# Seven block products for one more batch, x loaded batch by batch, and the first Wk load over two queues, in a cross-attention kernel

## The chip, the cores and the metric

The kernel runs on one core of a Trainium2 chip. The metric is device time in microseconds (us) for one execution. The engines of the core are named as the profile names them: PE (TensorE, matmuls), PEld (its weight loads), DVE (VectorE), ACT (ScalarE), POOL (GpSimd) and SP (SyncE, which here only issues DMAs). Each engine runs its own instructions strictly in the order in which the program wrote them, and waits where an instruction needs a result of another engine.

## The reference

Cross-attention of 16 batches of 256 rows (x, width 256) over 77 context keys each (width 192), with 8 heads of width 256, a residual and a layer norm. Everything is float32.

```python
Q = (img_embed @ Wq).reshape(B, -1, H, D).transpose(0, 2, 1, 3)
K = (sent_embed @ Wk).reshape(B, -1, H, D).transpose(0, 2, 1, 3)
V = (sent_embed @ Wv).reshape(B, -1, H, D).transpose(0, 2, 1, 3)
score = jnp.einsum('bhqd,bhkd->bhqk', Q, K) / math.sqrt(D)
score = jnp.where(mask, score, -jnp.inf)
attn = jax.nn.softmax(score, axis=-1)
ctx = jnp.einsum('bhqk,bhkd->bqhd', attn, V).reshape(B, -1, H * D)
out = ctx @ Wo + img_embed
# then layer norm over the last axis, with gamma and beta
```

## The kernel before

**Weights first.** The kernel never forms Q, K or V. It multiplies the weights of each head ahead of time: `gA`, `gB` hold Wk·Wqᵀ per head (the 192 context rows split 128 + 64, which is what A and B mean throughout), and `uA`, `uB` hold Wv·Wo. Per batch it then needs `a` (context times g: the keys as seen from x, `prepare_a`), and `vw` (context times u: the values as seen from the output, `prepare_vw`). The first part of the kernel, up to some 42 us, loads and turns the weights and builds g and u. All of its loads but half of Wv's stand in SP's queue in program order; the very first is `wk_nat` (Wk of the heads 0 and 1), then `wq_nat`, `wk_last`, `c_sb` (context) and blocks of Wq and Wk for the other heads.

**The main loop.** A tile is 128 rows of x; a batch is two tiles (2b and 2b+1), and four batches are a group g. The loop runs over `b` from -1 to 14, and I call one pass step b. Step b computes the scores and softmax of batch b+1 (its tiles are `new`), the output product of batch b (`now`), and the layer norm of batch b-1 (`old`). The order of calls in a step is the order of the instructions on each engine; the schedule is written out by hand, and no scheduler moves anything.

In a middle step, in order:

- `scores` (PE, L300) and `shift` (DVE, L317: adds the mask and takes the row minimum out of PSUM, eight per tile).
- In every second step (`ahead`), `prepare_vw` and `prepare_a` for the next two batches (PE, L190 to L235) and their copies out (ACT). In the steps 13 and 14 (`alone`) it is `prepare_vw` of the next batch only.
- `exponential` (ACT, L338), `finish` (DVE, L505 and L508: the statistics of an old tile), `weigh` (DVE L351 and L353, then POOL L359: divides by the denominators and writes `p`).
- `differences` (POOL, L412) and `sums` (POOL, L429 to L432): the sums and differences of blocks that the seven products need. `seven` (PE, L448) makes them, and an ACT copy (L473) brings four of them from PSUM to the tile `m`; `add_seven` (DVE L497, then five POOL additions, L483) puts the blocks together in `xg`, the tile that holds x and becomes the output.
- `turn` (DVE, L369: transposes `p` into `pT`), `normalise` (DVE L547 and L576, or with `aside` ACT L570 and POOL L571, L572), and the store (SP).

**Seven products or eight.** For one batch, `p` (two tiles) times `vw` is a 2×2 block product. `seven` does it with seven products of 128 output columns in place of eight, and needs `differences(b)` of `vw` and `sums(b)` of `pT` for that. `attend` (PE, L381) does the plain product, and needs neither. `NS` says which batches take which: the batches below NS, 13 before the change, take `seven`; the batches 13, 14 and 15 take `attend` (the very last tile `attend_halves`, L397). Two more things hang on NS. `vw` is kept as four blocks, and for the batches below NS one of them is the sum that `seven` reads in place of a plain block (`t2`). And `summed_by_act(t)` lets ACT sum the exponentials as it makes them (an accumulator read, L338), except for tiles from 2·NS up to 29, for which DVE does it (TENSOR_REDUCE, L351).

The four POOL operations of `sums` are in this order, and `seven` reads s2 in its second product:

```python
nc.gpsimd.tensor_tensor(s1, a2[0], a2[1], ALU.add)
nc.gpsimd.tensor_tensor(s3, a2[0], a1[0], ALU.subtract)
nc.gpsimd.tensor_tensor(s2, a2[1], s3, ALU.add)
nc.gpsimd.tensor_tensor(s4, a1[1], s2, ALU.subtract)
...
contract(pm[:, 0], *block(pT[0][:, 0:2], b11))
contract(pm[:, 1], *block(s2, t2))
```

**The last steps.** Step 13 calls `attend` for batch 13 and normalises batch 12 `aside`. Step 14 is written apart: it calls `shift` for tile 30, `finish` for tile 26, `shift` for tile 31, `finish` for tile 27, then the softmax of both tiles, `attend` for the tiles 28 to 30 and `attend_halves` for 31, with the last normalisations between them.

**Loads of x.** x comes twice: `load_x` brings rows into `xg` (for the residual), and `load_xT` brings 32×32 blocks into `xT`, which DVE transposes later (L162) for `scores`. Group g+1 is loaded while group g is worked on: `load_x` brings two batches (512 KB) in every second step, and `load_xT` one batch in four DMAs of 64 KB, twice. With `after_pool=True` a small POOL memset (L148) stands ahead of the load, and SP waits for that.

Of the kernel before, what the change touches and what calls it, by code (L numbers as in the profile page):

```python
# [16 lines left out]
P = 128  # L17
H = 8
D = 256
EPS = 1e-05  # L20
GB = 4
# [6 lines left out]
def kernel(  # L28
# [13 lines left out]
    nc = tc.nc  # L42
    B, S, DI = x.shape
# [3 lines left out]
    NG = B // GB  # L47
# [41 lines left out]
    NH = DI // 2 // BK  # L89
    uA = const.tile([P, 5, NH, NF, BK], F32, tag="uA", name="uA")  # L90
    uB = const.tile([P, 5, NH, NF, BK], F32, tag="uB", name="uB")
    NS = B - GB // 2 - 1

    def of_e(u, e):
        return u[:, 3 - 2 * e : 5 - 2 * e].rearrange("p q n i c -> p (q n) i c")
# [24 lines left out]
    def load_x(g, n=None, of=QT):  # L120
        if not n:
            xg_of[g] = const.tile([P, GT, DI], F32, tag=f"xg{g}", name=f"xg_{g}")
        lo, hi = (0, GT) if n is None else (n * QT, n * QT + of)
        nc.sync.dma_start(xg_of[g][:, lo:hi], x_rows[:, g * GT + lo : g * GT + hi, :])
# [17 lines left out]
    def load_xT(g, lo=0, hi=GT, after_pool=False):  # L142


        if lo == 0:
            xT_of[g] = in_two("xT", [P, GT * NM, 2, BK], g)
        if after_pool:
            nc.gpsimd.memset(xT_of[g][:BK, lo * NM, 0, :1], 0.0)  # L148
        rows = x.rearrange("b s d -> (b s) d")[(g * GT + lo) * P : (g * GT + hi) * P, :]
        rows = rows.rearrange("(m r) (i n) -> i r m n", r=BK, i=NM)  # L150
        for i in range(NM):
            nc.sync.dma_start(
                xT_of[g][i * BK : (i + 1) * BK, lo * NM : hi * NM].rearrange(
                    "p m n q -> p m (n q)"
                ),
                rows[i],
            )
# [218 lines left out]
    def attend(t):  # L376
        b, pT = t // QT, pT_of.pop(t)
        po = ps_mm.tile([P, DI], F32, tag="mm", name=f"po_{t}")
        for n in range(NF + 1):
            for i in range(NM):  # L380
                nc.tensor.matmul(  # L381
                    po[i * BK : (i + 1) * BK],
                    pT[:, n, i],
                    vw_of[b][:, 2 - n // 2 * 2 : 4 - n // 2 * 2, n % 2, :] if n < NF else vr[:, b, :],
                    start=(n == 0),
                    stop=(n == NF),
                )
        po_of[t] = po
# [46 lines left out]
    def seven(b):  # L435
        pT = [pT_of.pop(QT * b + i) for i in range(QT)]
        vw, ss = vw_of[b], ss_of.pop(b)
        ts = ts_of.pop(b)
        pm = ps_mm.tile([P, 4, P], F32, tag="mm", name=f"pm_{b}")
        po = ps_mm.tile([P, 4, P], F32, tag="mm", name=f"po_{b}")  # L440
        t2, b21, b22, b11 = (vw[:, q] for q in range(4))
        t4, t1, t3 = (ts[:, q] for q in range(3))
        s1, s3, s2, s4 = (ss[:, i] for i in range(4))

        def contract(out, *terms, first=True, final=True):
            for n, (weight, moving) in enumerate(terms):
                for i in range(NM):
                    nc.tensor.matmul(  # L448
                        out[i * BK : (i + 1) * BK],
                        weight[:, i],  # L450
                        moving,
                        start=first and n == 0,
                        stop=final and n == len(terms) - 1,
                    )

        def block(weights, moving):
            return [(weights[:, k], moving[:, k]) for k in range(2)]

        contract(pm[:, 0], *block(pT[0][:, 0:2], b11))
        contract(pm[:, 1], *block(s2, t2))  # L460
        contract(pm[:, 2], *block(s3, t3))
        contract(pm[:, 3], *block(s1, t1))
        for i in range(QT):
            contract(flat(po[:, 2 * i : 2 * i + 2]), (pT[i][:, NF], vr[:, b, :]), final=False)
            if i == 0:
                contract(po[:, 0], *block(pT[0][:, 2:4], b21), first=False, final=False)
                contract(po[:, 1], *block(s4, b22), first=False)
            else:
                contract(po[:, 2], *block(pT[1][:, 2:4], t4), first=False)
        for i in range(QT):  # L470
            po_of[QT * b + i] = flat(po[:, 2 * i : 2 * i + 2])
        m = vwp.tile([P, 4, P], F32, tag="m", name=f"m_{b}", bufs=1)
        nc.scalar.copy(m, pm)  # L473
        m_of[b] = m
# [127 lines left out]
    with tc.tile_pool(name="wonce", bufs=1) as wp:  # L602
# [39 lines left out]
            nc.gpsimd.tensor_copy(flat(cB)[:LB, rest], flat(cB)[LB:, rest])  # L642
            nc.gpsimd.tensor_copy(cRB, cB[:, :, KM:])

        nc.sync.dma_start(wk_nat, wk[:P, : 2 * D])
        for e in range(2):
            nc.sync.dma_start(wq_nat[:, :, e * D : (e + 1) * D], wq_rows[:, :, e * D : (e + 1) * D])
        for e in range(2):
# [304 lines left out]
    def work_of(b, rest_first=False):  # L953
        g, n = b // GB + 1, b % GB
        work = [prepare_vw(b, rest_first)]
        if g < NG - 1 or g == NG - 1 and n < NF // 2:
            work.append(prepare_a(g, (n,), rest_first=rest_first))
        elif b <= NS:
            part = (0, 2) if g < NG else (2, GB)
            work.append(prepare_a(NG - 1, (NF // 2 + n % 2,), *part, rest_first))  # L960
        return work
# [18 lines left out]
    for b in range(-1, B - 1):  # L980
        old = range(max(b - 1, 0) * QT, b * QT)
        now = range(max(b, 0) * QT, (b + 1) * QT)
        new = range((b + 1) * QT, (b + 2) * QT)
        for t in new if b >= 0 else ():
            scores(t)
        for t in new if b >= 0 else ():
            shift(t)
            if b == B - 2:
                finish(t - 2 * QT)
        while behind:  # L990
            behind.pop(0)()
        g, n = (b + 1) // GB + 1, (b + 1) % GB
        if g < NG and n % 2 == 0:
            load_x(g, n, 2 * QT)
        for m in range(0, 2) if b < 0 else range(b + 2, min(b + 3, B // 2)):
            turn_last(m)
        alone = b + 1 >= B - GB // 2
        works = work_of(b + 1) if alone or n % 2 == 0 else []
        for part_A, _, _ in works:
            part_A()  # L1000
        for _, part_B, _ in works:
            part_B()
        if b == B - 2:
            exponential(new[0])
            weigh(new[0])
            turn(new[0])
            spread(old[0], old[1] + 1)
            invert(old[0], old[1] + 1, aside=old[:1])
            normalise(old[1])
            exponential(new[1])  # L1010
            weigh(new[1])
            copy_out(works)
            normalise(old[0], aside=True)
            for t in now:
                attend(t)
            finish(now[0])
            centre(now[0])
            turn(new[1])
            scale_and_store(now[0])
            break  # L1020
        for i, t in enumerate(new if b >= 0 else ()):
            exponential(t)
            if old:
                finish(old[i])
            weigh(t)
        ahead = works and not alone
        if old and not ahead:
            spread(old[0], old[-1] + 1)
        if ahead:
            copy_out(works)  # L1030
            if old:
                spread(old[0], old[-1] + 1)
            works = work_of(b + 2, rest_first=True)
            for _, part_B, _ in works:
                part_B()
            for part_A, _, _ in works:
                part_A()
        copy_out(works)
        if b + 1 < NS:
            differences(b + 1)  # L1040
        if ahead and g < NG:
            load_xT(g, n * QT, (n + 1) * QT, after_pool=True)
        if b < NS:
            if now:
                seven(b)
            if old:
                invert(old[0], old[-1] + 1)
                normalise(old[0])
            for t in new:
                turn(t)  # L1050
            if b < 0:
                for j in range(QT, GT, 2):
                    transpose_x(0, j)
                bias_of(GB, B)
            if alone or ahead:
                turn_x_and_normalise(g, n, old)
                if ahead and g < NG:
                    load_xT(g, (n + 1) * QT, (n + 2) * QT)
            else:
                behind.append(partial(turn_x_and_normalise, g, n, old))  # L1060
            if ahead:
                sums(b + 1)
            if now:
                add_seven(b)
            if b + 1 < NS and not ahead:
                sums(b + 1)
            continue
        for t in now:
            attend(t)
        invert(old[0], old[-1] + 1, aside=old[:1])  # L1070
        normalise(old[0], aside=True)
        turn(new[0])
        normalise(old[1])
        turn(new[1])
        for t in now:
            add_product(t)


    attend(last - 1)
    attend_halves(last)  # L1080
# [40 lines left out]
```

## Time and profile before

| | |
|---|---|
| median of 3 runs | 270.57 us (270.32 to 271.32) |
| profiled execution, its own time | 270.98 us |
| span in that profile | 269.2 us |
| PE busy | 262.9 us (98%) |
| DVE busy | 185.2 us (69%) |
| POOL busy | 173.2 us (64%) |
| ACT busy | 157.7 us (59%) |
| granted TensorE clock | 1.0 throughout |
| DMA | 22.69 MB, mean 84 GB/s |

The span is measured from the first to the last instruction of the profiled execution; 1.78 us of its time lie outside. Busy shares are means over the whole span. The profile's chain of work is followed back from the last instruction, and shows what the end waited for at each point.

### The profile page before, as it was taken

What the parts mean: (1) busy time and instruction counts of PE and PEld (TensorE: products, weight loads), DVE (VectorE), ACT (ScalarE), POOL (GpSimd) and SP (SyncE); (2) the same over time, 40 slices, a digit from 0 to 9 for tenths busy, and PEclk for the clock granted to TensorE, in tenths of its full rate; (3) what the DMA queues carried; (4) which work ended last, traced back from release to release, by engine and by line L of the source; (5) the groups of instructions that cost most, each with busy time, mean ns of one, the idle gap of its engine ahead of it and who ended that gap; (6) DMA issues with size and microseconds to landing.
All of it is one profiled execution on the core that took longest, in us unless ns stands there. A gap on an engine that the chain in (4) does not pass through costs nothing.

```text
span 269.2 us, 14427 instructions
## 1 busy us (share of the span) xinstructions
PE 262.9 (98%) x6090; PEld 194.3 (72%) x6090; DVE 185.2 (69%) x808; ACT 157.7 (59%) x667; POOL 173.2 (64%) x240
## 2 busy tenths in 40 slices
PE   8999999999999999999999999999999999999993
PEld 7566598954985599459954995499769967984662
DVE  1555966483574758764896379647977897799785
ACT  3243335626857555964587377738684595636772
POOL 1042005637399647995699759965999799685462
PEclk9999999999999999999999999999999999999999
DMA  6999999901500130323022400340044010100112
GB/s 193 200 204 206 325 144 171 322 9 32 130 7 2 41 82 5 69 82 94 5 62 70 110 6 14 108 123 4 6 119 122 2 44 5 44 22 22 44 41 80
DMA packets 41616, 22.69 MB, mean 84 GB/s; under 512 B 24064, under 2 KB 40528, under 8 KB 41552
## 3 DMA queue, kind: packets, MB, share of 16 engines
q1 hardware_dynamic: 41168, 20.98, 32.7%
q0 software_dynamic: 384, 0.79, 1.4%
q8 instruction: 48, 0.79, 1.2%
q14 instruction: 16, 0.13, 0.2%
HBM read 17.57 MB, written 4.19 MB: 81 GB/s over the span
## 4 chain that ended last, share of the span: by engine, by line
PE 93%; DMA 3%; DVE 1%; SPq 1%; issue 0%; DVEq 0%
PE ps L300 25%; PE pa L190 12%; PE pv L224 11%; PE po L448 11%; PE pm L448 8%; PE pa L202 6%; PE pv L235 6%; PE po L381 4%; PE pu L777 3%; PE pr L260 2%; PE pgb L838 2%; DMA c_sb<-in_ctx_dram 2%; DMA wk_blk<-in_L_xattn_Wk_dram 2%; PE pw L791 1%; PE phb L854 1%; PE pr L271 1%
## 5 line engine op out<-in xcount | busy, mean ns | idle before, releaser
L338 ACT ACTIVATE e<-s,top 128x77 f32<-128x77 f32 x256 | 85.3, 346 | 44.5 <-DVE top L317 38.2
L300 PE MATMUL ps<-a,xT 128*32 128x154 f32 x2048 | 70.1, 294 | 0.0
L300 PEld LDWEIGHTS ps<-a,xT 128*32 128x32 f32 x2048 | 66.5, 110 | 1.1 <-issue 0.4
L359 POOL TENSOR_TENSOR p<-e,rden 128x512 f32<-128x512 f32 x64 | 47.5, 768 | 29.5 <-DVE rden L353 29.4
L317 DVE CUSTOM_DVE_ANT_0 s<-ps,bias 128x77 f32<-128x77 f32 x256 | 43.6, 232 | 14.8 <-PE ps L300 14.8
L338 ACT ACTIVATION_READ_ACCUMULATOR e<-s,top 128x1 f32 x224 | 42.0, 187 | 0.0
L190 PE MATMUL pa<-cA,gA 128*32 128x308 f32 (+1 forms) x576 | 36.8, 395 | 0.0
L190 PEld LDWEIGHTS pa<-cA,gA 128*32 128x32 f32 x576 | 19.0, 110 | 20.4 <-issue 6.7
L483 POOL TENSOR_TENSOR xg<-xg,m 128x256 f32<-128x256 f32 x39 | 28.7, 736 | 6.6 <-DVE xg L497 4.6
L576 DVE SCALAR_TENSOR_TENSOR xg<-xg,rstd,bet 128x256 f32<-128x256 f32 x27 | 22.2, 821 | 14.7 <-ACT rstd L527 13.3
L224 PE MATMUL pv<-uA,cA 128*32 128x512 f32 x256 | 30.8, 595 | 0.0
L412 POOL TENSOR_TENSOR ts<-vw 128x768 f32<-128x768 f32 x13 | 24.0, 1848 | 5.9 <-ACT vw L966 5.9
L369 DVE STREAM_TRANSPOSE pT<-p 128x640 f32<-128x640 f32 x32 | 25.5, 820 | 3.4 <-POOL p L359 3.3
L966 ACT COPY vw<-pv 128x512 f32<-128x512 f32 x32 | 17.8, 584 | 15.3 <-PE pv L224 8.1
L497 DVE TENSOR_TENSOR xg<-po,xg 128x256 f32<-128x256 f32 x31 | 11.5, 405 | 14.5 <-PE po L448 13.9
L317 DVE DVE_READ_ACCUMULATOR2_ANT top<- 128x1 f32 x256 | 20.8, 81 | 0.0
L202 PE MATMUL pa<-cB,gB 64*32 64x308 f32 (+2 forms) x512 | 20.4, 387 | 0.0
L966 ACT COPY a<-pa 128x308 f32<-128x308 f32 (+1 forms) x56 | 18.9, 395 | 1.9 <-PE pa L190 0.4
L202 PEld LDWEIGHTS pa<-cB,gB 64*32 64x32 f32 (+1 forms) x512 | 11.0, 110 | 11.4 <-issue 6.2
L547 DVE SCALAR_TENSOR_TENSOR xg<-xg,mv,gam 128x256 f32<-128x256 f32 x30 | 17.5, 585 | 0.1
L235 PE MATMUL pv<-uB,cB 64*32 64x512 f32 x256 | 17.3, 597 | 0.0
L224 PEld LDWEIGHTS pv<-uA,cA 128*32 128x32 f32 x256 | 8.0, 109 | 12.5 <-issue 9.5
(119 smaller groups left out, 407.6 us busy)
## 6 DMA issues: line engine op xcount, KB each, us to landing
xT<-in_x_dram SPq DMA_DIRECT2D x52, 64.0 KB, 2.4
xg<-in_x_dram SPq DMA_DIRECT2D x6, 512.0 KB, 4.2
out_dram<-xg SPq DMA_DIRECT2D x11, 256.0 KB, 2.3
wo<-in_L_xattn_Wo_dram SPq DMA_DIRECT2D x4, 512.0 KB, 8.9
wq_blk<-in_L_xattn_Wq_dram SPq DMA_DIRECT2D x12, 128.0 KB, 4.5
out_dram<-xg SPq DMA_DIRECT2D x10, 128.0 KB, 1.7
wk_blk<-in_L_xattn_Wk_dram SPq DMA_DIRECT2D x12, 96.0 KB, 4.3
xg<-in_x_dram SPq DMA_DIRECT2D x1, 1024.0 KB, 7.9
```

What stands on the lines that cost most here:

```text
L190: nc.tensor.matmul(flat(o[i * BK : (i + 1) * BK]), gA[:, h, cols(dc, i)], flat(cA[:, batches, :]), start=not rest_first and n in opening, ...
L202: nc.tensor.matmul(flat(banks[j + k][i * BK : (i + wide) * BK]), gB[half(k), h // 2, dc * P + i * BK : dc * P + (i + wide) * BK], flat(cB[ ...
L224: nc.tensor.matmul(pv[k][i * BK : (i + 1) * BK], cA[:, b, k * BK : (k + 1) * BK], uA[:, parts, :, i], start=not rest_first, stop=rest_first,)
L235: nc.tensor.matmul(pv[k][i * BK : (i + 1) * BK], cB[half(k), b, k * BK : (k + 1) * BK], uB[half(k), parts, :, i], start=rest_first, stop=n ...
L300: nc.tensor.matmul(ps[m // 2][i * BK : (i + 1) * BK, m % 2 * 2 * S2 : (m % 2 + 1) * 2 * S2], xT_of[g][:, j * NM + m, dc], flat(a_of[g][:, ...
L317: nc.vector.tensor_tensor_reduce(s[:, h], ps[a][:, k * S2 : (k + 1) * S2], bias[:, b, :], scale=-1.0, scalar=FAR, op0=ALU.add, op1=ALU.min ...
L338: nc.scalar.activation(e[:, h], s[:, h], AF.Exp, bias=top[:, one], scale=-1.0, accum_out=den[:, one] if summed_by_act(t) else None,)
L359: nc.gpsimd.tensor_tensor(part, e_mh[:, :, :, keys], rden_mh.unsqueeze(3).to_broadcast(list(part.shape)), ALU.mult,)
L369: nc.vector.transpose(pT_of[t].rearrange("p n m q -> p m n q"), p.rearrange("p m (n k) -> p m n k", k=BK),)
L448: nc.tensor.matmul(out[i * BK : (i + 1) * BK], weight[:, i], moving, start=first and n == 0, stop=final and n == len(terms) - 1,)
L483: nc.gpsimd.tensor_tensor(to, to, what, ALU.add)
L966: nc.scalar.copy(dst, src)
```

## The change

Three things change.

- `NS` goes from 13 to 14, so that batch 13 takes `seven` in place of `attend`. With it, step 12 gains `differences(13)` and `sums(13)`; step 13 gains `seven(13)` with its copy of `m`, and `add_seven(13)` at its end, in place of two `attend` and two `add_product`. The exponentials of the tiles 26 and 27 are now summed by ACT.
- `load_x` brings one batch (256 KB) at a time, before and after the first `load_xT` of the step; the first step's loads are x, xT, x for one batch each, of which the first xT load has no POOL memset ahead of it, and then the second batch's xT.
- The first load, `wk_nat`, is split by heads: one half is issued by SP, the other by ACT.

```diff
-    NS = B - GB // 2 - 1
+    NS = B - GB // 2
...
-        nc.sync.dma_start(wk_nat, wk[:P, : 2 * D])
+        for e, queue in enumerate((nc.sync, nc.scalar)):
+            queue.dma_start(wk_nat[:, e * D : (e + 1) * D], wk[:P, e * D : (e + 1) * D])
...
-        elif b <= NS:
+        elif b < NS:
...
         if g < NG and n % 2 == 0:
-            load_x(g, n, 2 * QT)
+            load_x(g, n)
+            if b < 0:
+                load_xT(g, n * QT, (n + 1) * QT)
+                load_x(g, n + 1)
...
         if ahead and g < NG:
-            load_xT(g, n * QT, (n + 1) * QT, after_pool=True)
+            m = n if b >= 0 else n + 1
+            load_xT(g, m * QT, (m + 1) * QT, after_pool=True)
+            if b >= 0:
+                load_x(g, n + 1)
         if b < NS:
             if now:
                 seven(b)
+            if b == NS - 1:
+                invert(old[0], old[-1] + 1, aside=old[:1])
+                normalise(old[0], aside=True)
+                turn(new[0])
+                normalise(old[1])
+                turn(new[1])
+                add_seven(b)
+                continue
...
-                if ahead and g < NG:
+                if ahead and g < NG and b >= 0:
                     load_xT(g, (n + 1) * QT, (n + 2) * QT)
...
-        for t in now:
-            attend(t)
-        invert(old[0], old[-1] + 1, aside=old[:1])
-        normalise(old[0], aside=True)
-        turn(new[0])
-        normalise(old[1])
-        turn(new[1])
-        for t in now:
-            add_product(t)
```

## The prediction, made before the changed kernel ran

> **What bounds the kernel now.** I read the page first, then the chain of work, then the timeline of the last 40 us engine by engine, because that is where NS acts.
>
> ```profile
> PE 262.9 (98%) x6090; PEld 194.3 (72%) x6090; DVE 185.2 (69%) x808; ACT 157.7 (59%) x667; POOL 173.2 (64%) x240
> ...
> PE 93%; DMA 3%; DVE 1%; SPq 1%; issue 0%; DVEq 0%
> ```
>
> The first line is busy time per engine, the second the shares of the chain that ended last. PE is the bound: it is busy for 262.9 of 269.2 us, and the chain runs over it for 93%. The chain of waits, in order of time, says from when to when:
>
> ```profile
> 7.99 4.34 DMA wk_blk<-in_L_xattn_Wk_dram
> ...
> 12.46 0.99 DVE kT L738
> ...
> 244.35 4.46 PE po L381 x80
> 248.80 4.19 PE ps L300 x128
> ```
>
> Up to 13.44 us loads set the pace; from 13.49 to 264.56 the chain is nearly all PE, `attend(13)` (L381, 80 records) included. So only two things can help: fewer PE instructions, or an earlier start. Anything that makes PE wait after 13.5 us is lost in full.
>
> How much PE work does batch 13 save? From the PE timeline:
>
> ```profile
> 233.32 0.62 PE L448 MATMUL pm<-vw,pT 128*32 128x128 f32 x16
> ...
> 237.24 4.37 PE L300 MATMUL ps<-a,xT 128*32 128x154 f32 x128
> ...
> 244.28 1.93 PE L381 MATMUL po<-vw,pT 128*32 128x256 f32 x32
> ...
> 248.62 4.37 PE L300 MATMUL ps<-a,xT 128*32 128x154 f32 x128
> ```
>
> `seven(12)` takes 237.24 - 233.32 = 3.92 us, `attend(13)` 248.62 - 244.28 = 4.34 us. The saving is 0.42 us, 0.16% of the time. It is easily lost again: `seven(13)` needs operands that POOL makes.
>
> **Change 1, batch 13: when are the sums ready?** Step 12 becomes what step 10 is now, with `differences`, `add_seven` and `sums` after its two `weigh`. Step 10 on POOL:
>
> ```profile
> 210.17 1.38 POOL L359 TENSOR_TENSOR p<-e,rden 128x512 f32<-128x512 f32 x2 [1.64 <-DVE rden L353]
> 211.84 1.69 POOL L359 TENSOR_TENSOR p<-e,rden 128x512 f32<-128x512 f32 x2 [0.29 <-DVE rden L353]
> 213.49 1.83 POOL L412 TENSOR_TENSOR ts<-vw 128x768 f32<-128x768 f32 x1
> 215.28 0.99 POOL L483 TENSOR_TENSOR m<-m 128x128 f32<-128x128 f32 x2
> 216.23 2.36 POOL L483 TENSOR_TENSOR xg<-xg,m 128x256 f32<-128x256 f32 x3
> 218.55 0.91 POOL L429 TENSOR_TENSOR ss<-pT 128x256 f32<-128x256 f32 x1
> 219.42 0.91 POOL L430 TENSOR_TENSOR ss<-pT,pT 128x256 f32<-128x256 f32 x1
> 220.41 0.73 POOL L431 TENSOR_TENSOR ss<-pT,ss 128x256 f32<-128x256 f32 x1
> 221.22 0.74 POOL L432 TENSOR_TENSOR ss<-pT,ss 128x256 f32<-128x256 f32 x1
> ```
>
> After these two steps PE starts the next scores at 212.40 and at 237.24, so step 12 lies 24.84 us after step 10. Adding that: POOL works almost without a gap from 235.0, s2 (L431) is done at 221.14 + 24.84 = 245.98, s4 (L432) at 246.80. The ACT accumulators for the tiles 26 and 27, and DVE's two TENSOR_REDUCE fewer, are in this copy already, since step 10 has them so.
>
> After step 10 the next `seven` comes late (225.4 us), because `prepare_vw` and `prepare_a` for two batches stand before it on PE. After step 12 only `prepare_vw(14)` does: PE reaches `seven(13)` at 244.28. Its first product (0.44 us; the four `pm` products of `seven(12)` take 1.74) ends at 244.72, the second needs s2. PE waits 245.98 + 0.06 - 244.72 = 1.32 us (0.06 for the step between engines, as the chain's "issue" pieces have it), and in strict order all of `seven(13)` and the scores of the tiles 30 and 31 wait behind it. These scores start at 244.28 + 3.92 + 1.32 = 249.52 instead of 248.62: 0.90 us later. The saving has become a loss.
>
> [...] The rows take 7.65 us for the same. I take the rows: two-input operations of 256 elements take 0.73 to 0.98 us in all 13 executions of `sums`.
>
> **Change 1, what follows on POOL and DVE.** In step 13 POOL goes straight from s4 to `weigh(28)`, `weigh(29)` (start 246.75, 2.97 us), `less` at 249.72, after 1.24 us (ACT's part between, as now from 248.91 to 250.15) L571 at 250.96, L572, and then the new `add_seven(13)` from 252.46. `m` is long there (the product ends near 247.5, an ACT copy takes 0.57 us). Two `m` operations (0.95) and three on `xg` (0.785 each): both halves of tile 26 are done at 254.98, all at 255.77.
>
> Who waits for that? In step 14 the statistics of tile 26 stand on DVE between `shift(30)` and `shift(31)`:
>
> ```profile
> 251.87 0.42 DVE L505 BATCH_NORM_STATS2 bn<-xg 128x6 f32<-128x256 f32 x1
> ...
> 253.69 0.42 DVE L505 BATCH_NORM_STATS2 bn<-xg 128x6 f32<-128x256 f32 x1
> ...
> 259.63 0.84 DVE L369 STREAM_TRANSPOSE pT<-p 128x640 f32<-128x640 f32 x1
> ```
>
> Now the first runs at 251.87 without a wait; it would run at 255.0, 3.1 us later. Behind it, with today's distances: `shift(31)` 255.57, second statistics 256.84, Ln on ACT 257.52, exponential of tile 31 from 257.95, its reciprocal 260.82, `weigh(31)` 261.14 to 262.52, `turn(31)` (the third line) 262.56 instead of 259.63. The copies of `vw(15)` queue behind that exponential and end at 261.73, so `attend(30)` starts at 261.75 (PE alone would be there at 260.89), `attend_halves` at 263.91, and PE ends at 266.28 instead of 264.52. DVE ends later still: after `turn(31)` it has two tiles of 1.54 us each, then 2.61 us from the first L515 to the end of L576. From 263.32 that is 269.01; today it ends at 266.55. So the end moves by 2.46 us, bound first by POOL, then by ACT and DVE. The 0.90 us of PE are contained in it, not added.
>
> **Change 2, loads of x.** Six more `load_x` issues of about 0.45 us (L124) make 2.7 us on SP's queue, spread over four steps; the bytes are the same. SP stands waiting most of the time (84 us for normalised rows at L584 alone, 44 us for the memsets at L148). The later halves of x stand behind `load_xT` and its wait, but `xg` is read four steps after it is loaded, tens of us, and no engine's wait list names an x load. The first xT load of step -1 now waits for POOL till 63.73 and would go at about 49, into a DMA system that is full until about 50 and 5% busy from 58 to 66. Cost 0; if that cover failed, an `xg` load (4.2 us to landing) would show as a DVE wait at L497.
>
> **Change 3, Wk over two queues.** SP issues one half where it issued the whole (128 rows each, 0.39 us), so nothing behind it moves; ACT issues the other half ahead of its table load, which ends at 2.03 us now, and ACT's first copy comes at 4.80: 0.4 us of issue is covered. Both halves use the same DMA engines as what follows, with a share of 0.92 from 3.0 to 6.7 us. No row shows a split, so both ends: 128 more packets over 16 engines at the mean of 34 ns (32.7% of 16 × 269.2 us over 41,168 packets) cost 8 × 34 = 0.27 us at most; a gain is at most the 8% of these 3.7 us that are free, 0.3 us. PE's first transposes are not the limit anyway, since the Wq loads (5.61), c_sb (7.97) and wk_blk (12.33) follow. I take 0, and keep -0.3 and +0.3. [...]
>
> **Sum.** +2.46 + 0 + 0 against the profiled execution (270.98 us, span 269.2), that is 273.4; on the median, which is 0.41 us lower, 270.57 + 2.46 = 273.0 us.
>
> **The rivals.**
>
> *POOL is in time* (chance 0.06). If s2 is done by 244.7, 1.3 us sooner than the copy of step 10 says, PE saves its 0.42 us and `add_seven(13)` ends early enough to delay `turn(31)` within its slack (it ends at 260.47, PE needs it at 262.15). The time would be 270.2 to 270.7: not slower. [...] Against: steps 8 and 10 place s2 alike, 16.9 us after the start of their scores, and with every sum at its shortest row (0.73) only 0.4 us are found.
>
> *Only PE's wait counts* (0.08). If DVE and ACT absorb the late statistics, 0.90 us remain: 271.5, within what cannot be told apart. It needs `add_seven(13)` done on tile 26 by 252.8, 2.2 us sooner. Against: POOL has almost no gap there.
>
> *The start slips too* (0.05). The Wk halves delay c_sb and with it wk_blk by 0.3 us; PE's start has only 0.19 us of wait: 273.3. If also the statistics of tile 26 wait for the last of the five additions, 0.79 us more: 274.1.
>
> **How the numbers follow.** The main case has 0.81. About 0.5% (1.35 us) is what a measurement of this kernel can tell from no change, so slower means over 271.9: main case and slipping start, 0.86. Same: 0.12, from the other two rivals. Faster by 0.5% would need 1.35 us, and 0.42 + 0.3 do not make it: 0.02. The range goes from PE's wait alone (271.5, rounded down to 271.4) to the slipping start with the longer wait (274.1, 274.2).
>
> **What would show it.** Right: a PE wait of about 1.3 us at L448 before the products with `ss` in step 13, the first in the chain; a DVE wait of about 2 to 3 us at L505 for POOL L483 near 253; POOL without a gap from 235 to 250; and DVE, not PE, ending last by over 2 us. Wrong: no PE wait at L448 near 245, or statistics of tile 26 near 252; then the time is under 271. PE's first L854 matmuls should start within 0.3 us of 13.49; beyond that, change 3 was mis-sized.

## The result, and the profile after

The changed kernel takes 273.18 us (median of 6 runs, 272.85 to 274.23), the kernel before 270.64 us (6 runs, 270.32 to 271.32). The ratio is 1.010, with a 95% interval from 1.0086 to 1.0113: 2.5 us slower. The profiled execution takes 273.67 us with a span of 271.8 us, 2.6 us longer than before. Its granted TensorE clock is 0.996 in the mean, where before has 1.0; that is no part of the loss, because step 12 begins at the same time in both (see below).

The page after, its busy times and the shares of its chain of work:

```profile
PE 263.4 (97%) x6138; PEld 194.4 (72%) x6138; DVE 184.4 (68%) x806; ACT 159.1 (59%) x684; POOL 180.9 (67%) x250
...
PE 74%; DMA 10%; POOL 4%; DVE 4%; ACT 4%; issue 1%; SPq 1%; DVEq 0%; POOLq 0%; ACTq 0%
```

POOL has 7.7 us more to do (173.2 before), ACT 1.4 us, DVE 0.8 us less. The busy time of PE does not show what batch 13 saved: it is 0.5 us more. The second line is the one to read. Before, the chain was 93% PE; now POOL, DVE and ACT have 4% each, some 32 us together. Read in order of time, the chain leaves PE near 230.4 us, in the scores of step 12, and comes back to it only from 261.09 to 264.88, in the last products. (The 10% DMA are the start: in this execution the chain runs over the loads of Wv and Wo, and PE waited 0.61 us for Wo at 32.45 us. It is no part of the loss, because PE starts the scores of step 12 at 229.10 us here and at 229.13 before.) PE's wait in step 13, shown below, does not lie on the chain.

The waits of the stretch from 228 to 272 us (waited for: total us, times, longest us):

```profile
DVE bn L505 <- POOL xg L483: 2.2, 1, 2.2
...
PEld pm L448 <- POOL ss L431: 1.4, 1, 1.4
...
PE pm L448 <- POOL ss L431: 1.1, 1, 1.1
```

Both waits are new, and POOL is what they wait for. The timeline of PE shows the first one in place:

```profile
244.24 0.64 PE L448 MATMUL pm<-vw,pT 128*32 128x128 f32 x16
245.98 0.64 PE L448 MATMUL pm<-vw,ss 128*32 128x128 f32 x16 [1.09 <-POOL ss L431]
...
249.48 4.37 PE L300 MATMUL ps<-a,xT 128*32 128x154 f32 x128
...
261.09 1.98 PE L381 MATMUL po<-vw,pT 128*32 128x256 f32 x32
...
263.54 1.08 PE L397 MATMUL po<-vw,pT 128*32 128x128 f32 x32
```

`seven(13)` starts where `attend(13)` did (244.28 before), loses 1.3 us after its first product (these products follow each other at 0.44 us, so the second was due at 244.68; the row counts 1.09 from the end that the profile models for the first), and the next scores come at 249.48 instead of 248.62. The timeline of POOL says why, and leads to the second wait:

```profile
238.29 1.83 POOL L412 TENSOR_TENSOR ts<-vw 128x768 f32<-128x768 f32 x1
240.09 0.98 POOL L483 TENSOR_TENSOR m<-m 128x128 f32<-128x128 f32 x2
241.03 2.35 POOL L483 TENSOR_TENSOR xg<-xg,m 128x256 f32<-128x256 f32 x3
243.34 0.92 POOL L429 TENSOR_TENSOR ss<-pT 128x256 f32<-128x256 f32 x1
244.22 0.90 POOL L430 TENSOR_TENSOR ss<-pT,pT 128x256 f32<-128x256 f32 x1
245.20 0.72 POOL L431 TENSOR_TENSOR ss<-pT,ss 128x256 f32<-128x256 f32 x1
...
252.30 0.99 POOL L483 TENSOR_TENSOR m<-m 128x128 f32<-128x128 f32 x2
253.25 2.35 POOL L483 TENSOR_TENSOR xg<-xg,m 128x256 f32<-128x256 f32 x3
```

Each row starts where the one before ended: POOL has a queue, not a slow operation. The last two rows are `add_seven(13)`, which follows the softmax of batch 14 and the normalisation of tile 24. On DVE the statistics of tile 26 wait for its second `xg` addition:

```profile
254.82 0.43 DVE L505 BATCH_NORM_STATS2 bn<-xg 128x6 f32<-128x256 f32 x1 [2.21 <-POOL xg L483]
...
262.55 0.84 DVE L369 STREAM_TRANSPOSE pT<-p 128x640 f32<-128x640 f32 x1 [0.26 <-POOL p L359]
...
268.59 0.48 DVE L576 SCALAR_TENSOR_TENSOR xg<-xg,rstd,bet 128x256 f32<-128x256 f32 x1
```

Against before, the statistics are 2.95 us later (251.87), `turn(31)` 2.92 us (259.63) and the last operation of DVE 2.52 us (it ended at 266.55, now at 269.07). The 0.4 us between the last two are mostly waits for PE that DVE had after `turn(31)` before (0.32 us of it at L497 for tile 30) and now has not: DVE runs without a gap from `turn(31)` to the end.

### The profile page after: what moved, and what is told of

Same layout as the page of the kernel before. It is cut to its first block, busy times and chain, and to the rows that moved or that the text cites. A ratio compares the mean times of both kernels' runs of the same rounds, so it can differ in the third digit from the quotient of the medians.

```text
span 271.8 us, 14561 instructions
## 1 busy us (share of the span) xinstructions
PE 263.4 (97%) x6138; PEld 194.4 (72%) x6138; DVE 184.4 (68%) x806; ACT 159.1 (59%) x684; POOL 180.9 (67%) x250
## 4 chain that ended last, share of the span: by engine, by line
PE 74%; DMA 10%; POOL 4%; DVE 4%; ACT 4%; issue 1%; SPq 1%; DVEq 0%; POOLq 0%; ACTq 0%
PE ps L300 21%; PE po L448 10%; PE pv L224 9%; PE pa L190 9%; PE pm L448 8%; PE pv L235 5%; PE pa L202 5%; DMA wk_blk<-in_L_xattn_Wk_dram 3%; ACT e L338 3%; DMA wvT<-in_L_xattn_Wv_dram 3%; PE pu L778 3%; DMA wo<-in_L_xattn_Wo_dram 3%; PE pr L260 2%; DMA wq_blk<-in_L_xattn_Wq_dram 2%; POOL xg L483 1%; PE pw L792 1%
## 5 line engine op out<-in xcount | busy, mean ns | idle before, releaser
L338 ACT ACTIVATE e<-s,top 128x77 f32<-128x77 f32 x256 | 86.6, 346 | 43.7 <-DVE top L317 40.7
L338 ACT ACTIVATION_READ_ACCUMULATOR e<-s,top 128x1 f32 x240 | 44.8, 187 | 0.0
L483 POOL TENSOR_TENSOR xg<-xg,m 128x256 f32<-128x256 f32 x42 | 30.9, 736 | 5.8 <-DVE xg L497 3.6
L190 PEld LDWEIGHTS pa<-cA,gA 128*32 128x32 f32 x576 | 18.4, 110 | 20.9 <-issue 6.9
L576 DVE SCALAR_TENSOR_TENSOR xg<-xg,rstd,bet 128x256 f32<-128x256 f32 x27 | 22.9, 849 | 14.3 <-ACT rstd L527 12.9
L412 POOL TENSOR_TENSOR ts<-vw 128x768 f32<-128x768 f32 x14 | 25.9, 1847 | 5.9 <-ACT vw L967 5.9
L369 DVE STREAM_TRANSPOSE pT<-p 128x640 f32<-128x640 f32 x32 | 25.5, 821 | 4.2 <-POOL p L359 4.2
L497 DVE TENSOR_TENSOR xg<-po,xg 128x256 f32<-128x256 f32 x31 | 11.4, 403 | 13.4 <-PE po L448 13.4
L547 DVE SCALAR_TENSOR_TENSOR xg<-xg,mv,gam 128x256 f32<-128x256 f32 x30 | 17.8, 593 | 0.1
L448 PE MATMUL po<-vr,pT 128*32 128x256 f32 x224 | 17.3, 379 | 0.0
```

Source lines behind the costliest of these rows:

```text
L190: nc.tensor.matmul(flat(o[i * BK : (i + 1) * BK]), gA[:, h, cols(dc, i)], flat(cA[:, batches, :]), start=not rest_first and n in opening, ...
L338: nc.scalar.activation(e[:, h], s[:, h], AF.Exp, bias=top[:, one], scale=-1.0, accum_out=den[:, one] if summed_by_act(t) else None,)
L412: nc.gpsimd.tensor_tensor(ts.rearrange("p q k d -> p q (k d)"), vw[:, 1:4], vw[:, 0:1].to_broadcast([P, 3, 2 * P]), ALU.subtract,)
L448: nc.tensor.matmul(out[i * BK : (i + 1) * BK], weight[:, i], moving, start=first and n == 0, stop=final and n == len(terms) - 1,)
L483: nc.gpsimd.tensor_tensor(to, to, what, ALU.add)
```

## The experiments

Each kernel was timed beside the kernel before on the same chip. The kernel before took 270.46 us beside e1 to e4, 270.68 beside e5 to e8, 270.71 beside e9 to e11 and 270.66 beside e12.

My theory was the prediction's: the whole loss is batch 13, and within it the late `add_seven(13)` sets the size, while PE's wait for s2 is hidden behind it. The rivals were that the loads carry a part, and that PE's wait is what counts.

### One part alone: e1, e2, e3

e1 is the kernel before with only the batch changed, e2 with only the loads of x as in the change, e3 with only the split of Wk.

```diff
 e1
-    NS = B - GB // 2 - 1
+    NS = B - GB // 2
...
+            if b == NS - 1:
+                invert(old[0], old[-1] + 1, aside=old[:1])
...
 e3
-        nc.sync.dma_start(wk_nat, wk[:P, : 2 * D])
+        for e, queue in enumerate((nc.sync, nc.scalar)):
+            queue.dma_start(wk_nat[:, e * D : (e + 1) * D], wk[:P, e * D : (e + 1) * D])
```

> Only the first of the three edits (batch 13 takes the seven products); loads as before. Theory (POOL is late for batch 13): all of the loss is here, time +2.4 to +2.6 us against the kernel before, with a PE wait of 1.1 to 1.4 us before the second product of seven(13) and a DVE wait of about 2.2 us at L505 for tile 26. Rival (the loads make part of the loss, by the later Wo landing that the changed kernel shows): +1.5 to +2.0 us here.

> Only the second edit (x one batch at a time, first step's loads in three parts). Theory: 0 (within 0.3 us of before), and no engine waits for an x load. Rival (loads cost): +0.5 us or more.

> Only the third edit (first Wk load over SP's and ACT's queues). Theory: 0 to +0.3 us; the start of the L854 matmuls moves from 13.49 to at most 13.8. Rival (the 0.6 us that PE waits for Wo in the changed kernel comes from here and stays): +0.5 to +0.9 us. A gain would be at most 0.3 us.

| kernel | time, us | ratio to before, 95% |
|---|---|---|
| e1, batch 13 | 273.10 | 1.0099 [1.0086, 1.0111] |
| e2, loads of x | 270.72 | 1.0010 [1.0001, 1.0018] |
| e3, Wk split | 270.98 | 1.0016 [1.0008, 1.0025] |

e1 alone has the ratio of the whole change, and both waits (1.11 us at L448, 2.21 us at L505); its 2.64 us are just over the 2.6 expected. The loads of x cost what was expected, within 0.3 us.

The split of Wk alone cost 0.52 us by the medians (0.43 by the ratio), more than the 0.3 that I had allowed. The start does not show it. PE's L854 matmuls begin at 13.97 us in e3, later than the 13.8 that I expected; but they begin at 13.49 to 13.99 us in the seven kernels with the old load, and at 13.59 to 14.06 in the seven with the split, so these times cannot be told apart. The end does show it. From the end of DVE's last operation to the end of the span, e3 takes 3.07 us and the kernel before 2.64, 0.43 less. There SP waits for the last store (first row before, second e3):

```profile
SPq L1116 <- DMA out_dram<-xg: 0.9, 1, 0.9
...
SPq L1117 <- DMA out_dram<-xg: 1.3, 1, 1.3
```

In both kernels this wait ends 1.38 us after the store was issued, and it is one of nine semaphores that SP checks there in turn. Before, it is the ninth, and the other eight are checked while the store is under way. In e3 it is the second, and seven checks of 0.06 us each come after it. In the whole change it is the eighth, and the same stretch takes 2.70 us. So in the one trace of each, the order of these checks accounts for e3's loss, and the whole change does not have it. Why the order differs is not shown.

### PE's wait taken away: e4 and e6

e4 puts `sums(13)` on POOL ahead of `add_seven(12)`, so that s2 is ready earlier. e6 leaves POOL alone and lets `seven(13)` start with the products that need no sums.

```diff
 e4
-            if ahead:
+            if ahead or b == NS - 2:
                 sums(b + 1)
             if now:
                 add_seven(b)
-            if b + 1 < NS and not ahead:
+            if b + 1 < NS - 1 and not ahead:
                 sums(b + 1)
...
 e6
         contract(pm[:, 0], *block(pT[0][:, 0:2], b11))
+        if b == NS - 1:
+            contract(flat(po[:, 2:4]), (pT[1][:, NF], vr[:, b, :]), final=False)
+            contract(po[:, 2], *block(pT[1][:, 2:4], t4), first=False)
+            contract(flat(po[:, 0:2]), (pT[0][:, NF], vr[:, b, :]), final=False)
+            contract(po[:, 0], *block(pT[0][:, 2:4], b21), first=False, final=False)
         contract(pm[:, 1], *block(s2, t2))
...
```

> The changed kernel with sums(13) ahead of add_seven(12) on POOL in step 12, so that s2 is done near 242.7 instead of 245.9. Theory (the end is set by POOL, then DVE and ACT): the PE wait at L448 goes, but POOL does the same work up to add_seven(13), so the time stays within 0.4 us of the changed kernel (273.0 to 273.6). Rival (PE's wait is what counts): the time falls by 0.9 to 1.3 us, to 271.9 to 272.3.

> The changed kernel with the products of seven(13) in another order: those that need no sums first (2.2 us), so that PE has work until s2 is done. POOL is not touched. Theory: PE's wait of 1.1 to 1.3 us at L448 goes, and the time stays within 0.3 us of the changed kernel, since the end waits for POOL, DVE and ACT. Rival (PE's wait counts): 271.9 to 272.3.

e6 took 273.13 us (1.0101 [1.0077, 1.0125]), the time of the whole change. Its products (PE) and the weight loads of `attend(30)` (PEld):

```profile
246.00 0.62 PE L448 MATMUL pm<-vw,ss 128*32 128x128 f32 x16
...
260.69 1.98 PE L381 MATMUL po<-vw,pT 128*32 128x256 f32 x32 [1.38 <-DVE xg L504]
```

```profile
260.69 0.16 PEld L381 LDWEIGHTS po<-vw,pT 128*32 128x32 f32 x8 [1.86 <-ACT vw L974]
261.17 1.02 PEld L381 LDWEIGHTS po<-vw,pT 128*32 128x32 f32 x24 [0.32 <-ACT vw L974]
```

The product with s2 no longer waits, and PE stands for 1.38 us in front of `attend(30)` instead. The row of PE names an addition of DVE, which ends at that time; the weight loads name what `attend(30)` reads, the two ACT copies of `vw(15)` (from 260.08 for 1.04 us). So PE's wait at L448 was hidden, as the prediction had it: it is contained in the 2.5 us and not added to them.

e4 took 274.07 us (1.0132 [1.0118, 1.0146]), 0.9 us over the whole change. PE's wait was gone and the time did not fall, so the rival was refuted here too, but I had expected a difference within 0.4 us. Its DVE timeline shows what I had left out:

```profile
245.06 0.43 DVE L505 BATCH_NORM_STATS2 bn<-xg 128x6 f32<-128x256 f32 x1 [1.85 <-POOL xg L483]
...
254.99 0.43 DVE L505 BATCH_NORM_STATS2 bn<-xg 128x6 f32<-128x256 f32 x1 [2.22 <-POOL xg L483]
```

The statistics of tile 24 stand in step 13 as those of tile 26 stand in step 14, and now wait 1.85 us for the `add_seven(12)` that was pushed back. DVE's denominators of tile 28 stand behind them, so `weigh(28)` waits on POOL for 0.93 us, and with it everything that follows. It is the wait of the change, made twice.

### `add_seven(13)` sooner: e5

e5 moves the `aside` normalisation of tile 24 (ACT L570, POOL L571 and L572) behind `add_seven(13)`.

```diff
-                normalise(old[0], aside=True)
                 turn(new[0])
                 normalise(old[1])
                 turn(new[1])
                 add_seven(b)
+                normalise(old[0], aside=True)
                 continue
```

> The changed kernel with one call moved: normalise(old[0], aside) of step 13 comes after add_seven(13), so that POOL's five additions for batch 13 no longer stand behind the wait for ACT and the two operations L571 and L572. Tile 26 is whole near 252.6 instead of 254.8, and DVE's wait at L505 shrinks from 2.2 to about 0.1 us. Theory: the end is bound by PE again, and only PE's wait before seven(13)'s sums is left, about +0.9 us against the kernel before: 271.3 to 271.7. Rival (DVE's wait is not what sets the end): within 0.3 us of the changed kernel, 273.2.

e5 took 271.70 us (1.0042 [1.0026, 1.0057]), as expected: 1.0 us over before. Its DVE and PE timelines:

```profile
253.19 0.43 DVE L505 BATCH_NORM_STATS2 bn<-xg 128x6 f32<-128x256 f32 x1
```

```profile
246.49 0.64 PE L448 MATMUL pm<-vw,ss 128*32 128x128 f32 x16 [1.09 <-POOL ss L431]
```

The wait at L505 is gone, that of PE is still there, and what is left of the loss is what PE alone would lose: counted from the scores of step 12, DVE ends 0.91 us later than before. This is the prediction's second rival, produced by hand: once the statistics come in time, PE's wait is what counts.

### Both waits taken away: e7 and e8

e7 has the edits of e5 and e6; e8 is e7 with the old loads of x and Wk.

> Both moves of the last two experiments together. Theory: neither wait is left and the 0.42 us of PE work are gained, with 0 to 0.3 us for the start: 270.1 to 270.5, against 270.6 before. Rival (something else in the change costs): 271 or more.

> As the last one, with the loads of x and Wk as in the kernel before. Theory: 270.0 to 270.3, 0.3 to 0.5 us under the kernel before. Rival (the new loads help): slower than the last one.

e7 took 271.02 us (1.0016 [1.0009, 1.0023]), e8 270.86 us (1.0008 [1.0002, 1.0015]). Neither is faster than before, though both waits are gone. Two of my expectations missed by half a microsecond, so the 0.4 us that PE saves had to be somewhere. Rows of PE and of DVE in e8:

```profile
228.41 4.37 PE L300 MATMUL ps<-a,xT 128*32 128x154 f32 x128
...
263.00 0.40 PE L397 MATMUL po<-vr,pT 128*32 128x128 f32 x8
```

```profile
259.75 0.84 DVE L369 STREAM_TRANSPOSE pT<-p 128x640 f32<-128x640 f32 x1 [0.26 <-POOL p L359]
...
265.80 0.48 DVE L583 SCALAR_TENSOR_TENSOR xg<-xg,rstd,bet 128x256 f32<-128x256 f32 x1
```

I read three times from the start of step 12's scores, so that the start of the kernel drops out:

| us after the start of the scores of step 12 | before | e8 |
|---|---|---|
| PE's last product ends | 35.39 | 34.99 |
| `turn(31)` starts | 30.50 | 31.34 |
| DVE's last operation ends | 37.42 | 37.87 |

PE does end 0.40 us sooner: the saving is there. But `turn(31)` is 0.84 us later, and DVE, which has the last word, ends 0.45 us later. In e8 the chain of work leaves PE near 229.7 us and does not come back to it: it ends over POOL's sums, `add_seven(13)`, the softmax of tile 31 and DVE.

### The last step: e9 to e12

If the start of `turn(31)` sets the end, an earlier exponential of tile 31 should free PE's 0.4 us. e9 is e8 with step 14 reordered: both `shift`s first, the exponential of tile 31 straight behind that of tile 30, and the statistics of the tiles 26 and 27 after both. e10 is the same reordering on the kernel before, e11 on e7.

```diff
-            if b == B - 2:
-                finish(t - 2 * QT)
...
             weigh(new[0])
-            turn(new[0])
+            exponential(new[1])
+            finish(old[0])
+            finish(old[1])
             spread(old[0], old[1] + 1)
+            turn(new[0])
+            weigh(new[1])
+            copy_out(works)
             invert(old[0], old[1] + 1, aside=old[:1])
             normalise(old[1])
-            exponential(new[1])
-            weigh(new[1])
-            copy_out(works)
             normalise(old[0], aside=True)
             for t in now:
                 attend(t)
+            turn(new[1])
             finish(now[0])
             centre(now[0])
-            turn(new[1])
```

> The kernel before with batch 13 in seven products, seven(13)'s sums-free products first, the aside part of normalise(26 - 2) behind add_seven(13) (the kernel of e8), and in step 14 both shifts ahead of the statistics of the tiles 26 and 27, and the exponential of tile 31 straight behind that of tile 30. My theory: in e8 the saving of PE (0.40 us, measured from the scores of step 12) is there, but the end follows DVE: turn(31) starts at 259.75 and the add of tile 30 (the third from the last) starts 0.8 us after PE had its product. With the exponential of tile 31 moved from 254.93 to about 253.6, turn(31) starts near 258.5 to 259.0, DVE waits for PE again at the add of tile 30, and the end is PE's: 0.6 to 0.8 us under e8, 270.0 to 270.3 where before is 270.7. Rival: the end of e8 is set by the amount of DVE's work after turn(31) and not by its start; then nothing changes (270.7 to 270.9).

> The kernel before with the reordered step 14 alone (control for e9). In the kernel before DVE waits 0.32 us for PE at the add of tile 30, so its end is PE's already, and an earlier turn(31) buys nothing: 0 within 0.2 us. If it gains as much as e9 does, the gain of e9 belongs to the reordering and not to the seven products.

> The whole change with the three repairs of e9 (new loads of x, Wk over two queues, seven products for batch 13). If the loads cost what e3 and the starts of PE's first products say (0.2 to 0.5 us), it lies 0.2 to 0.5 us over e9: 270.2 to 270.8. If they cost nothing, as the prediction had it, it equals e9 within 0.15.

e9 took 271.67 us (1.0045 [1.0028, 1.0063]), e10 271.24 (1.0016 [1.0005, 1.0027]), e11 271.97 (1.0050 [1.0031, 1.0070]). All three missed (e11 did lie 0.30 us over e9, within the 0.2 to 0.5 expected): the reordering made both kernels slower. `turn(31)` did come sooner, in e9 by 1.26 us against e8 (30.08 after the scores of step 12), in e10 by 1.13 us against before (29.37), but DVE ended 0.73 and 0.47 us later. So the theory that the start of `turn(31)` sets the end falls. I had moved the add, the statistics and the centring of tile 28 behind it, 1.5 us of DVE's work before and 1.9 us here, and DVE had no gap left behind `turn(31)`.

e12 repairs that: `finish(28)` and `centre(28)` stand ahead of `turn(31)` again, and the centring of tile 27 goes into the gap ahead of `turn(30)`.

```diff
             spread(old[0], old[1] + 1)
+            centre(old[1])
             turn(new[0])
...
-            normalise(old[1])
+            normalise(old[1], centred=True)
...
-            turn(new[1])
             finish(now[0])
             centre(now[0])
+            turn(new[1])
```

> The kernel of e9 with two steps moved on DVE: centre(27) ahead of turn(30), into the 0.66 us in which DVE waits for weigh(30), and finish(28) with centre(28) ahead of turn(31) again, as the kernel before has them. e9 and e10 moved turn(31) 1.1 to 1.3 us earlier against the scores of step 12 and still ended DVE 0.5 to 0.7 us later, since 1.9 us of DVE's work had moved behind turn(31). My theory now: the end is set by how much of DVE's work stands behind PE's last products; with finish(28) and centre(28) back in front and 0.44 us more in the gap, DVE catches up with PE before the halves of tile 31 and the end is PE's last product plus 2.03 us: 1.2 to 1.6 us under e9, 270.1 to 270.5 where before is 270.7. Rival: DVE's additions lengthen beside POOL's work (SCALAR_TENSOR_TENSOR 0.88 and 1.09 us in e9 where 0.48 is the shortest), so that it never catches up with PE: then 270.8 to 271.3.

e12 took 270.86 us (1.0012 [1.0004, 1.0020]): the rival's end. From the scores of step 12 PE ends at 34.99 us as in e8, `turn(31)` starts at 31.26, and DVE ends at 37.81. The chain of e12, in order of time:

```profile
251.02 5.59 ACT e L338 x32
256.62 0.20 ACT log L533
...
256.84 0.21 ACT rstd L534
...
257.07 1.26 DVE xg L583
258.34 0.34 DVE xg L504
...
259.87 0.76 DVE pT L369
```

The two exponentials now stand ahead of the `rstd` of tile 27, and the operation that needs it takes 1.26 us, where it takes 0.48 with no POOL addition beside it. On POOL `weigh(31)` runs at that time:

```profile
257.00 1.56 POOL L359 TENSOR_TENSOR p<-e,rden 128x512 f32<-128x512 f32 x2 [1.04 <-DVE rden L353]
```

After that DVE has no gap until the end. No order of step 14 that I tried gives it one, and no version beats the kernel before.

## Why the prediction was right

**PE's saving and its wait.** The page's pieces say 3.94 us for `seven(13)` without its wait (249.48 - 244.24 - 1.30), 3.92 was taken. The wait, counted as in the prediction from the end of the first product (244.68), is 1.30 us where 1.32 was said, and the next scores start at 249.48 where 249.52 was said.

**The copy of step 10.** It held to 0.1 us: L412 at 238.29 (238.33), s2 done at 245.92 (245.98), s4 at 246.73 (246.80). From the start of L412 to the end of s2 it took 7.63 us, where the rows of step 10 have 7.65.

**POOL, then DVE.** `weigh(28)` began at 246.69 (246.75), `add_seven(13)` at 252.30 (252.46), the statistics of tile 26 at 254.82 (255.0), `weigh(31)` at 260.89 (261.14), `turn(31)` at 262.55 (262.56), and DVE ended at 269.07 (269.01). That the last of these is within 0.1 us is in part luck, because some terms were off and cancelled. `attend(30)` started at 261.09, 0.66 us sooner than said: it needs only the first of the two copies of `vw(15)` to begin, and it then waits for the second, so that it takes 2.45 us where 2.16 was used. And `weigh(31)` took 1.63 us where 1.38 was used, which used up the 0.25 us that it had begun sooner. After `turn(31)` DVE's three terms were 1.59, 1.69 and 2.47 us where 1.54, 1.54 and 2.61 were used. PE's end (265.94, said 266.28) did not decide, as said.

**That PE's 0.90 us are contained in the 2.46.** e6 shows it: without that wait the time is the same.

**PE as the bound.** The prediction's opening went too far with "anything that makes PE wait after 13.5 us is lost in full": in e6 the 1.30 us of wait are gone and nothing is won, and in e8 PE ends 0.40 us sooner and the kernel does not. In the last steps DVE decides. The number did not suffer, because the sum followed POOL and DVE there.

**The loads.** 0 was taken for both. In the kernels that have batch 13 too, the two load edits together cost from 0.03 us (the change against e1, by their ratios) over 0.16 (e7 against e8) to 0.30 (e11 against e9), which is within the bounds that were kept. Alone, e2 and e3 cost 0.26 and 0.52 us, and the second lies outside: the prediction looked for a cost at the start, and in e3's trace it came at the end, in the order of SP's last checks. No gain from the second issuer was seen in e3.

**The rivals.** "POOL is in time" was wrong: POOL had no gap over 0.3 us between 235 and 250 us. Its time of 270.2 to 270.7 is doubtful too: e7, in which both waits for POOL are gone, took 271.02 us. "Only PE's wait counts" came true where its condition was made true, in e5, at 271.7 us; the prediction had 271.5. Of "the start slips too" nothing was seen: L854's matmuls began at 13.74 us instead of 13.49, within the spread of the kernels with the old load, and step 12 began as before. One of the signs, "DVE, not PE, ending last by over 2 us", could not tell the cases apart: DVE ended 3.13 us after PE here, but 2.03 us after it already before.

## What to carry to other kernels

A trick that takes 0.4 us of matmuls off one engine and gives another almost 8 us of additions pays only where the second has that much idle time before its results are needed; near the end of a kernel there is no later work to hide it behind. Follow an addition to the queue of every engine that waits for it: here the products of `seven(13)` that need no sums stood behind PE's wait of 1.09 us at L448 (in e6 they ran ahead of the product with s2), and a statistic that nobody was in a hurry for stood, with its wait of 2.21 us, in front of the softmax of the last tile. And before an engine is relieved, see which engine ends next: DVE waited only 0.3 to 0.4 us for PE at the end, so hardly more than that was to be won from PE.

## What the runs showed of the hardware

In the traces an operation of DVE with two SBUF inputs is often longer beside a two-input operation of POOL. SCALAR_TENSOR_TENSOR (L547 and L576, 256 elements, both inputs in SBUF) runs 57 times in the trace of before. 23 of these take 0.43 to 0.49 us, among them all 7 that have no such POOL operation beside them. The other 34 take 0.55 to 1.37 us, and every one of them ends 0.28 to 0.29 us after the end of a POOL operation that ran beside it. POOL's operation can be longer there too: L429 of step 12 takes 0.92 us in the change, where such an operation of DVE runs beside it, and 0.73 in e4, where DVE reads the scores from PSUM at that time.

Operations of DVE with only one input in SBUF do not show this. In the trace of before, the statistics (L505) take 0.38 to 0.42 us with no POOL operation beside them and 0.38 to 0.43 with one all the time, the transposes (L369) 0.80 to 0.85 in both cases, and the additions from PSUM (L497) 0.38 to 0.43 in both.

The 1.26 us of e12 look the same: the first operation of `weigh(31)` began 0.07 us ahead of DVE's and ended at 258.06, and DVE's ended at 258.34. What makes them longer is not shown: no run here took one of the two away. If it is POOL's work, then that work is paid for a second time on DVE, and in e12 it is paid on the chain that ends last: 0.78 us, by 1.26 against 0.48.
